# Three seams of a graph network kernel: first loads over other tiles between two stages, a new order in the third pass, and half of the head's sums kept in PSUM

## The chip, the core and the metric

One core of a Trainium2 chip runs the whole program. The metric is the device time of one execution in microseconds (us). The profile shows five engines beside each other: PE (TensorE, matrix products), DVE (VectorE), ACT (ScalarE), POOL (GpSimd) and SP (SyncE, which here only issues DMAs). PEld are PE's weight loads.

## What is computed

16 graphs of 1024 nodes with 128 channels pass two layers. The first layer runs four rounds of message passing with a GRU cell (`h = gru(adj.T @ (h @ W), h)`), adds the input and normalises each row. The second layer thins each adjacency by a row-by-row neighbour skipping, and runs three graph convolutions with a batch norm over all nodes of all graphs behind each of them:

```
adj_d = adj * keep(adj)                      # the skipping, row after row
def sage(x):  out = (adj_d @ x / deg) @ Wr + x @ Wx + b;  return out / norm(out) * mask
h1 = bn(relu(sage1(x)));  h2 = bn(relu(sage2(h1)));  h3 = bn(relu(sage3(h2)))
y  = (concat(h1, h2, h3) @ Wl + bl) * mask
out = layernorm(x + y)
```

Each batch norm needs all 16 graphs, so the convolutions are three passes over all graphs, and a head behind them.

## The kernel before

**First stage, to about 1334 us.** `Gated` (the GRU layer, two graphs in turn as two streams) and `FixPoint` (the skipping) run interleaved: `Gated.layer` calls `aside(n)` at fixed places, and each of these calls lets one piece of the skipping run. `Gated.layer` ends with the cell's last products: `zh = z*h` and `h = zh - r` on POOL (lines 1112, 1116, 1118) and a DVE step between them (L1117). After the last layer `finish` turns the state on PE (L1025), scales it on ACT (L1055), adds the input on POOL (L1057) and stores the sum from POOL's queue (L1059). The skipping leaves its rows in the DRAM tensor `e_nr`.

**First pass (`Sage.first`), about 1349 to 1900 us.** For each graph, 16 slots (`slot(b, t)`). A slot does one `unit` of the next graph n = b+1 (PE turns and combines pieces of the adjacency `p_a` and the skipping's rows `p_nr` into `p_u`, L1464 to L1471, and ACT evicts to `p_at`, L1472), a `pack` of it on POOL (L1479), and a share of the products of graph b (`agg`, L1543). Graph -1 is a lead-in: its 16 slots only prepare graph 0. `check` (L1488) looks at an adjacency tile on DVE; `norm_stats` and `norm` (L1497 to L1509) normalise the summed rows `p_s`, `turn_x` (L1402) turns them on PE, and `split` (L1396, L1397) cuts them in a high and a low part on ACT and POOL. Rows come by SP's queue: `load_a` (L1440), `load_nr` (L1448), `load_s` (L1454).

**Between them.** The constructor `Sage.__init__` loads weights, ten rows of vectors (L1228 to L1236) and three copies of the node mask (L1276), computes small constants on DVE and POOL, corrects the first weight by a product on PE (L1259), and turns the vectors (L1241). `run` then makes the first bias rows (`weights(0)`, L1344 and `parts`, L1320 to L1327) before `first` begins.

**Second pass**, to about 2171 us. **Third pass (`third`)**: 32 units of half a graph. In iteration i, `out_next(i)` makes three products on PE (L1734, L1737, L1740), `rows(i-2)` scales a result on DVE (L1386 to L1391), `chain(i)` scales on ACT (L1370), adds on DVE (L1373) and takes sums of squares on ACT (L1380, L1381), a DVE addition collects the head's part (L1833), and the result of i-3 is turned on PE (L1402), copied by ACT (L1837) and summed up by DVE's `bn_stats` (L1838).

**Head (`last`)**: `head_weights` makes one row `r48` for all graphs; for each graph, two halves of four products with the mask rows (L1864) and four with `r3` (L1867) in a PSUM tile; DVE adds `acc` (L1869), takes statistics (L1872, L1874), ACT a root (L1876), DVE the factors (L1881, L1882), and ACT writes eight normalised blocks (L1885) for one store of 512 KB (L1887). `norm(b-1)` comes after `head(b)`.

What sets the order: inside a stage the text of the program is the order of each engine's queue (`manual_schedule`); code outside of these sections, and two such sections towards each other, are placed by a planner. Tiles live in pools that are laid one behind the other in SBUF; a pool that opens over a closed one's space waits, tile by tile, for whoever still uses the old tiles there. DMAs of one queue are issued in order.

Of the kernel before, what the change touches and what calls it, by code (L numbers as in the profile page):

```python
# [21 lines left out]
P = 128  # L22
# [894 lines left out]
class Gated:  # L917
# [7 lines left out]
    def __init__(self, ctx, tc, cst, x, adj, weight, w_ih, w_hh, b_ih, b_hh, summed):  # L925
        self.tc, self.nc, self.cst = tc, tc.nc, cst
        self.x, self.adj, self.summed = x, adj, summed
        nc = self.nc
        pool = lambda name, **k: ctx.enter_context(tc.tile_pool(name=name, **k))
        self.one = pool("h_one", bufs=1)  # L930
        self.adjp = pool("h_adj", bufs=NB)
        self.wk = pool("h_wk", bufs=2)

        self.ps6 = pool("h_ps6", bufs=6, space=PSUM)
        self.wi = self.one.tile([C, L0, 3, C], F32, name="h_wi")
        self.wh = self.one.tile([C, L0, 3, C], F32, name="h_wh")
        self.bi = self.one.tile([C, L0 * 3], F32, name="h_bi")
        self.bh = self.one.tile([C, L0 * 3], F32, name="h_bh")
        self.bs = self.one.tile([C, L0 * 3], F32, name="h_bs")
        self.given = weight, w_ih, w_hh, b_ih, b_hh  # L940
# [50 lines left out]
    class Stream:  # L991
# [56 lines left out]
        def finish(self, f):  # L1048
# [8 lines left out]
            nc.gpsimd.tensor_tensor(x[:, rows, :], x[:, rows, :], y, ALU.add)  # L1057
# [3 lines left out]
    def layer(self, st, l, aside):  # L1061

        nc, wk = self.nc, self.wk
        half = [slice(f * HF, (f + 1) * HF) for f in range(2)]
# [28 lines left out]
        for f in range(2):  # L1093
# [17 lines left out]
            if f == 0:  # L1111
                nc.gpsimd.tensor_tensor(zh, z, h, ALU.mult)  # L1112
                aside(6)
        for f, (r, z, zh, h) in enumerate(rest):
            if f == 1:
                nc.gpsimd.tensor_tensor(zh, z, h, ALU.mult)
            nc.vector.scalar_tensor_tensor(r, z, 1.0, r, op0=ALU.subtract, op1=ALU.mult)  # L1117
            nc.gpsimd.tensor_tensor(h, zh, r, ALU.subtract)  # L1118
# [75 lines left out]
class Sage:  # L1194
# [14 lines left out]
    def __init__(self, ctx, tc, cst, adj, not_r, summed, nodemask, W, vec, Wl, bl, out, bad):  # L1209
        self.tc, self.nc, self.cst = tc, tc.nc, cst  # L1210
        self.adj, self.not_r, self.summed, self.out, self.bad = adj, not_r, summed, out, bad
        nc, ident = self.nc, cst["ident"]
# [10 lines left out]

        self.wr = one.tile([C, 3, C], F32, name="s_wr")
        self.wx = one.tile([C, 3, C], F32, name="s_wx")
        self.wl = one.tile([C, 3, C], F32, name="s_wl")
        for i in range(3):
# [3 lines left out]

        vr = one.tile([10, C], F32, name="s_vr")
        row = lambda v: v.rearrange("(o c) -> o c", o=1)
        for i, v in enumerate(vec):
            nc.sync.dma_start(vr[i:i + 1, :], row(v))
        nc.sync.dma_start(vr[9:, :], row(bl))  # L1236
        self.vr = vr
        self.vt = one.tile([C, 10], F32, name="s_vt")
        with tc.tile_pool(name="s_ps0", bufs=1, space=PSUM) as ps:
            pv = ps.tile([C, 10], F32, name="s_v")  # L1240
            nc.tensor.transpose(pv, vr, ident[:10, :10])  # L1241
            nc.vector.tensor_copy(self.vt, pv)
        const = lambda shape, v, name, dt=F32: self.const(shape, v, name, dt)
        self.eps = const([P, 1], 1e-5, "s_eps")
        self.less2 = const([P, 1], -2.0, "s_less2")
# [6 lines left out]
        with tc.tile_pool(name="s_wk1", bufs=1) as wk, tc.tile_pool(name="s_ps1", bufs=1, space=PSUM) as ps:  # L1252

            drop = wk.tile([C, C], F32, name="s_drop")
            nc.vector.tensor_copy(drop, ident)
            nc.vector.memset(drop[:1, :], -1.0)
            nc.vector.memset(drop[:1, :1], 0.0)
            w = ps.tile([C, C], F32, name="s_w1")
            nc.tensor.matmul(w, drop, self.wr[:, 0, :], start=True, stop=True)  # L1259
            nc.vector.tensor_copy(self.wr[:, 0, :], w)  # L1260
        self.part6 = one.tile([6, 3], F32, name="s_part6")
        nc.vector.tensor_add(self.part6, ident[:6, 0:3], ident[:6, 3:6])

        K = 3 * B
# [4 lines left out]
        self.graph = one.tile([K, B], F32, name="s_graph")  # L1269
        nc.vector.tensor_add(self.graph, ident[:K, :B], ident[:K, B:2 * B])  # L1270
        nc.vector.tensor_add(self.graph, self.graph, ident[:K, 2 * B:K])
        self.mask48 = one.tile([K, N], BF, name="s_mask48")
        with tc.tile_pool(name="s_wk0", bufs=1) as wk:
            m = wk.tile([K, N], F32, name="s_m48")
            for i in range(3):
                nc.sync.dma_start(m[i * B:(i + 1) * B, :], nodemask)  # L1276
            nc.vector.tensor_copy(self.mask48, m)
            o = wk.tile([B, N], BF, name="s_o16")
            nc.vector.memset(o, 1.0)
            for i in range(3):  # L1280
                nc.sync.dma_start(self.rho[:, 3 + i, :], o)

            junk = wk.tile([P, NB, B], F32, name="s_mjunk")
            mask = cst["mask"]
            nc.vector.scalar_tensor_tensor(junk, mask, 0.0, mask, op0=ALU.is_gt, op1=ALU.not_equal,
                                           accum_out=bad[:, BAD - 1:BAD])
        self.rdeg = one.tile([P, B, NB], F32, name="s_rdeg")
        self.stats = [one.tile([C, 2 * B, 6], F32, name=f"s_st{l}") for l in range(3)]
        self.ab = [one.tile([C, 2], F32, name=f"s_ab{l}") for l in range(3)]
        self.wr2 = one.tile([C, C], F32, name="s_wr2")  # L1290
        self.wxp = one.tile([C, 2, C], F32, name="s_wxp")
        self.r6 = one.tile([6, 2 * C], BF, name="s_r6")
        nc.vector.memset(self.r6[:, C:], 0.0)
# [35 lines left out]
    def weights(self, l, ps):  # L1329

        nc = self.nc
        v = ps.tile([6, C], F32, name="s_v6")
# [73 lines left out]
    def first(self):  # L1406

        nc, tc, cst = self.nc, self.tc, self.cst
        with ExitStack() as c:
            pool = lambda name, **k: c.enter_context(tc.tile_pool(name=name, **k))  # L1410
            self.wk = pool("p_wk", bufs=2)
            self.big = pool("p_at", bufs=2)
            self.ap = pool("p_a", bufs=8)
# [4 lines left out]
            c.enter_context(tc.manual_schedule(engines={ET.PE, ET.DVE, ET.Activation, ET.Pool, ET.SP}))  # L1418

            xp = pool("p_x", bufs=1)  # L1420
# [4 lines left out]
            self.g = {}  # L1425
            for k in range(4):
                self.load_a(0, k)
            for f in range(2):
                self.load_nr(0, f)
            self.load_s(0)  # L1430
            for k in range(4):
                self.check(0, k)
# [4 lines left out]
    def load_a(self, b, k):  # L1437
        if b < B:
            t = self.ap.tile([P, N], F32, name="p_a")
# [3 lines left out]
    def load_nr(self, b, f):  # L1443
        if b < B:
            g = self.g.setdefault(b, {})
            if f == 0:
                g["nr"] = self.big.tile([P, NB, N], BF, name="p_nr")
            self.nc.sync.dma_start(g["nr"][:, 4 * f:4 * f + 4, :], rows_of(self.not_r[b, f * HF:(f + 1) * HF, :]))  # L1448

    def load_s(self, b):  # L1450
        if b < B:
            g = self.g.setdefault(b, {})
            g["s"] = self.wk.tile([P, NB, C], F32, name="p_s")
            self.nc.sync.dma_start(g["s"], self.summed[b])  # L1454

    def unit(self, b, t):

        nc, g, f, j = self.nc, self.g[b], t // 8, t % 8
        if t == 0:
            g["at"] = self.big.tile([P, NB, N], FR, name="p_at")  # L1460
# [121 lines left out]
    def slot(self, b, t):  # L1582
# [4 lines left out]
        if nxt:  # L1587
            if t < 4:
# [52 lines left out]
        if nxt:  # L1641
# [6 lines left out]
            if t in (7, 12):  # L1648
                self.split_x(n, t // 12)
            if t in (4, 5, 10, 11):  # L1650
# [12 lines left out]
        if nxt:  # L1663
            if t == 10:
                nc.sync.dma_start(self.at8[n, 0], self.g[n]["b", 0])
            if t == 13:
                nc.sync.dma_start(self.x1[n], self.g[n]["s"])
        if t == 1 and b >= 1:
# [137 lines left out]
    def third(self):  # L1806

        nc, tc = self.nc, self.tc
        with ExitStack() as c:
# [10 lines left out]
            for i in range(len(units) + 3):  # L1820
                if i < len(units):
# [4 lines left out]
                if 2 <= i < len(units) + 2:  # L1826
                    b1, f1 = units[i - 2]
                    g = self.g[b1]
                    g["r", f1] = self.rows(b1, f1, g.pop(("o", f1)), g.pop(("ss", f1)))
                if i < len(units):  # L1830
# [3 lines left out]
                if i >= 3:  # L1834
                    b2, f2 = units[i - 3]
                    pt = self.turned(self.g[b2]["r", f2], self.ps2)
                    nc.scalar.copy(self.r3[:, b2, f2, :], pt)  # L1837
                    nc.vector.bn_stats(self.stats[2][:, 2 * b2 + f2, :], self.r3[:, b2, f2, :])  # L1838


    def last(self, r48):
        nc, tc, cst = self.nc, self.tc, self.cst
        with ExitStack() as c:
            pool = lambda name, **k: c.enter_context(tc.tile_pool(name=name, **k))
            wk = pool("u_wk", bufs=6)
            ps = pool("u_ps", bufs=4, space=PSUM)
# [3 lines left out]
            def row(b):  # L1850
                if b < B:
                    st["row", b] = wk.tile([3 * B, C], BF, name="u_rb", bufs=3)
                    nc.vector.tensor_scalar(st["row", b], r48, self.graph[:, b:b + 1], None, op0=ALU.mult)

            def head(b):
                rb = st.pop(("row", b))
                row(b + 1)
                y = wk.tile([P, NB, C], F32, name="u_y")
                mv = self.small.tile([P, NB, 2], F32, name="p_mv")
                for f in range(2):  # L1860
                    pp = ps.tile([P, 4, C], F32, name="u_p")
                    for i in range(4):
                        k = 4 * f + i
                        nc.tensor.matmul(pp[:, i, :], self.mask48[:, k * P:(k + 1) * P], rb,  # L1864
                                         start=(i == 0), stop=False)
                    for i in range(4):
                        nc.tensor.matmul(pp[:, i, :], self.r3[:, b, f, i * P:(i + 1) * P], self.wr2,  # L1867
                                         start=False, stop=(i == 3))
                    nc.vector.tensor_add(y[:, 4 * f:4 * f + 4, :], pp, self.acc[:, b, 4 * f:4 * f + 4, :])  # L1869
                    s6 = self.small.tile([P, 4, 6], F32, name="p_st")  # L1870
                    for i in range(4):
                        nc.vector.bn_stats(s6[:, i, :], y[:, 4 * f + i, :])  # L1872
# [4 lines left out]
                st[b] = y, mv, rs  # L1877

            def norm(b):
                y, mv, rs = st.pop(b)  # L1880
# [3 lines left out]
                for k in range(NB):  # L1884
                    nc.scalar.activation(y[:, k, :], y[:, k, :], AF.Identity, bias=rs[:, 1, k:k + 1],  # L1885
                                         scale=rs[:, 0, k:k + 1])
                nc.sync.dma_start(rows_of(self.out[b]), y)  # L1887

            row(0)
            for b in range(B + 1):  # L1890
# [5 lines left out]
    def run(self):  # L1896
        tc, nc = self.tc, self.nc
        with tc.tile_pool(name="s_psw", bufs=1, space=PSUM) as ps:
            self.weights(0, ps)
        self.first()  # L1900
        with tc.tile_pool(name="s_psw", bufs=1, space=PSUM) as ps:
            self.weights(1, ps)
# [4 lines left out]
        with tc.tile_pool(name="s_psw", bufs=1, space=PSUM) as ps:  # L1907
            self.weights(2, ps)
# [93 lines left out]
```

## Time and profile before

| what | us |
|---|---|
| median of 3 runs (2422.9 to 2429.3) | 2425.41 |
| the profiled execution | 2424.86 |
| its span, first to last instruction | 2423.1 |
| PE / DVE / ACT / POOL busy in it | 2260.7 / 1927.9 / 1384.0 / 1014.2 |
| mean granted clock of TensorE | 0.98 |

The page of the profile gives busy time by engine, 40 slices of the span, the chain of work that ended last, and groups by line. Other views answer questions on a stretch: a table by windows (busy time of each engine, granted clock, share and rate of the DMAs), a timeline (start, duration, engine, line, operation, and in brackets how long the engine had been idle before it and what ended that), and the waits. "x4" is four instructions merged in one line; a matrix product of 32-bit floats shows as two records. Times in the timeline count from the span's start.

### The profile page before, as it was taken

The numbers are of one execution on the slowest core, as the hardware profiler recorded it, in microseconds if no ns is written. First come the engines' busy times: TensorE is split into PE (matmuls) and PEld (weight loads), VectorE is DVE, ScalarE is ACT, GpSimd is POOL, SyncE is SP. The second block draws the span as 40 slices with busy tenths as digits, with TensorE's granted clock in tenths as the row PEclk, the third lists the DMA queues.
The fourth block names the chain that finished last, engine by engine and source line by source line (L and its number), as shares of the span: only waits on it lengthen the run. The fifth ranks groups of instructions, "written<-read, shape, count | busy, mean of one in ns | idle before, by whom it ended". The sixth has DMA issues, their size and how long they took to land.

```text
span 2423.1 us, 35665 instructions
## 1 busy us (share of the span) xinstructions
PE 2260.7 (93%) x11897; PEld 1558.2 (64%) x11913; DVE 1927.9 (80%) x4153; ACT 1384.0 (57%) x3228; POOL 1014.2 (42%) x937
## 2 busy tenths in 40 slices
PE   6999999999999999999998699999999899989875
PEld 4666555666556656566555477777777677777654
DVE  4998998989989989899899677777777466665677
ACT  3566556565565555565655466665666354545647
POOL 3335244353352442533523566666666244440000
PEclk9999999999999999999999799999999899999988
DMA  7337253364271643632722777887775466645404
GB/s 257 110 99 256 68 207 125 124 226 125 90 245 57 224 132 118 217 119 95 260 69 84 280 274 269 295 287 282 269 271 216 173 234 223 232 149 172 123 9 132
DMA packets 214389, 436.17 MB, mean 180 GB/s; under 512 B 59570, under 2 KB 80724, under 8 KB 214196
## 3 DMA queue, kind: packets, MB, share of 16 engines
q1 hardware_dynamic: 186756, 345.96, 41.5%
q0 software_dynamic: 23040, 83.90, 10.2%
q10 hardware_dynamic: 4400, 3.95, 0.5%
q8 instruction: 96, 1.57, 0.3%
q14 instruction: 97, 0.79, 0.1%
HBM read 324.49 MB, written 109.25 MB: 179 GB/s over the span
## 4 chain that ended last, share of the span: by engine, by line
PE 49%; DVE 22%; ACT 12%; DMA 8%; issue 6%; POOL 3%; SPq 0%; DVEq 0%; ACTq 0%; POOLq 0%
PE h_g L1089 12%; PE p_ag L1543 9%; PE h_g L1077 9%; DVE f_rank L735 4%; DMA e_sum<-h_x 3%; ACT s_junk L1380 2%; PE q_ag L1776 2%; PE p_u L1470 2%; PE p_u L1471 2%; PE p_u L1464 2%; ACT f_u L909 2%; DMA h_a<-in_adj_dram 2%; DVE f_x L893 2%; PE q_ob L1740 2%; PE s_tr L1402 1%
## 5 line engine op out<-in xcount | busy, mean ns | idle before, releaser
L1089 PE MATMUL h_g<-h_h,h_wh 128*128 128x512 f32 x768 | 397.7, 599 | 3.6 <-DVE h_r L1102 3.5
L1089 PE MATMUL h_g<-h_ms,h_wi 128*128 128x512 f32 x768 | 392.3, 592 | 0.0
L1479 POOL CAST p_b<-p_at 128x512 uint8<-128x512 f32 x256 | 256.3, 1021 | 129.5 <-ACT p_at L1472 129.4
L735 DVE TENSOR_TENSOR_SCAN f_rank<-f_a,f_first,f_pd 128x1024 f16<-128x1024 f32 x128 | 299.3, 2344 | 3.3
L1077 PE MATMUL h_g<-h_a,h_hi 128*128 128x512 f32 x1024 | 284.0, 417 | 7.5 <-DMA h_a<-in_adj_dram 7.4
L1118 POOL TENSOR_TENSOR h_h<-h_zh,h_r 128x512 f32<-128x512 f32 x128 | 184.7, 1443 | 198.1 <-DVE h_r L1117 170.7
L1472 ACT ACTIVATE p_at<-p_u,s_less 128x512 fp32r<-128x512 f32 x256 | 175.9, 688 | 157.9 <-PE p_u L1471 154.3
L1089 PEld LDWEIGHTS h_g<-h_ms,h_wi 128*128 128x128 f32 x768 | 145.5, 190 | 184.3 <-issue 164.2
L1077 PE MATMUL h_g<-h_a,h_lo 128*128 128x512 f32 x1024 | 262.0, 393 | 0.0
L1077 PEld LDWEIGHTS h_g<-h_a,h_hi 128*128 128x128 f32 x1024 | 188.3, 188 | 71.5 <-issue 20.3
L863 DVE SCALAR_TENSOR_TENSOR f_nr<-f_u,f_q,f_a 128x1024 bf16<-128x1024 f16 x128 | 183.8, 1453 | 57.1 <-ACT f_u L912 50.4
L1112 POOL TENSOR_TENSOR h_zh<-h_z,h_h 128x512 f32<-128x512 f32 x64 | 81.6, 1275 | 323.7 <-ACT h_z L1108 323.7
L1077 PEld LDWEIGHTS h_g<-h_a,h_lo 128*128 128x128 f32 x1024 | 189.9, 188 | 38.3
L1488 DVE SCALAR_TENSOR_TENSOR p_a<-p_a 128x1024 bf16<-128x1024 f32 x128 | 209.9, 1679 | 3.1 <-DMA p_a<-in_adj_dram 3.1
L1380 ACT ACTIVATE s_junk<-s_o 128x128 bf16<-128x128 f32 x384 | 113.7, 298 | 128.7 <-DVE s_o L1373 128.7
L1089 PEld LDWEIGHTS h_g<-h_h,h_wh 128*128 128x128 f32 x768 | 129.1, 190 | 86.7 <-issue 68.3
L1105 ACT ACTIVATE h_r<-h_r,h_bi 128x512 f32<-128x512 f32 x128 | 92.4, 722 | 140.8 <-DVE h_r L1104 140.8
L1080 ACT COPY h_ms<-h_g 128x512 f32<-128x512 f32 x128 | 73.9, 577 | 173.0 <-PE h_g L1077 129.9
L909 ACT ACTIVATE f_u<-f_rank,f_q 128x128 f16<-128x128 f16 (+7 forms) x128 | 110.6, 867 | 75.1 <-DVE f_rank L849 75.1
L1470 PE MATMUL p_u<-ident_b,p_a 128*128 128x128 bf16 x1024 | 144.9, 222 | 4.0 <-DMA p_a<-in_adj_dram 3.0
L1471 PE MATMUL p_u<-ident_b,p_nr 128*128 128x128 bf16 x1024 | 144.9, 222 | 0.0
L1740 PE MATMUL q_ob<-s_wxp,q_xt 128*128 128x256 f32 x512 | 130.8, 399 | 0.0
(243 smaller groups left out, 4942.2 us busy)
## 6 DMA issues: line engine op xcount, KB each, us to landing
h_a<-in_adj_dram POOLq DMA_DIRECT2D x128, 512.0 KB, 7.4
p_a<-in_adj_dram SPq DMA_DIRECT2D x128, 512.0 KB
f_a<-in_adj_dram SPq DMA_DIRECT2D x124, 512.0 KB
e_nr<-f_nr SPq DMA_DIRECT2D x128, 256.0 KB
p_nr<-e_nr SPq DMA_DIRECT2D x32, 1024.0 KB
s_at<-p_b SPq DMA_DIRECT2D x32, 512.0 KB
s_ag<-s_ag SPq DMA_DIRECT2D x64, 256.0 KB
q_agi<-s_ag SPq DMA_DIRECT2D x32, 512.0 KB
```

Of the source, the lines that this page charges most:

```text
L735: nc.vector.tensor_tensor_scan(out, a, other[:, 0, 0:1].to_broadcast([P, N]), start, op0=ALU.add, op1=ALU.bypass)
L863: nc.vector.scalar_tensor_tensor(nr, self.us[g], self.q[:, 2, g:g + 1], self.a[g], op0=ALU.not_equal, op1=ALU.is_ge)
L1077: nc.tensor.matmul(pm[f], part[:, j, :], st.adj[j][:, half[f]], start=(j == 0 and n == 0), stop=(j == NB - 1 and n == 1))
L1089: nc.tensor.matmul(pg, lhs, rhs, start=(i == 0), stop=(i == len(mm) - 1))
L1118: nc.gpsimd.tensor_tensor(h, zh, r, ALU.subtract)
L1470: nc.tensor.matmul(pu[:, i * P:(i + 1) * P], a[:, blk, 1], ib, start=False, stop=False)
L1471: nc.tensor.matmul(pu[:, i * P:(i + 1) * P], nr[:, k, blk], ib, start=False, stop=(i == 3))
L1472: nc.scalar.activation(g["at"][:, j, cols], pu, AF.Relu, bias=self.less2)
L1479: self.nc.gpsimd.tensor_copy(g["b", f][:, j, :], g["at"][:, j, f * HF:(f + 1) * HF].bitcast(F32))
L1488: self.nc.vector.scalar_tensor_tensor(low, a, 0.0, a, op0=ALU.is_gt, op1=ALU.not_equal, accum_out=self.bad[:, c:c + 1])
L1543: self.nc.tensor.matmul(pa, hi[:, j, :], at[:, j, f * HF:(f + 1) * HF], start=(start and n == 0), stop=(stop and n == len(js) - 1))
L1740: nc.tensor.matmul(pb[:, i], g["xt"][:, f, blk], self.wxp, start=False, stop=(i % 2 == 1))
```

## The change

Five things change. **(a)** `h_adj` is laid out ahead of `h_one`, and the pools of the first pass are split and ordered anew, so that the first rows' tiles (`p_nr0`, `p_a0`, `p_nr1`, `p_a1`) lie over the skipping's tiles and the rest over the adjacency of the GRU. The first loads stand at the head of `first` in one order on SP. **(b)** The constructor only makes tiles. Its loads stand behind the first rows (`load_given`); the constants come in the lead-in's slot 9 (`constants`), and the products with the weights, the vectors and `weights(0)` at the end of slot (0, 1) (`first_weights`). The first four `check`s move from ahead of the slots into slots 0 to 3 of the lead-in. **(c)** In the very last GRU layer, and in the last `finish`, POOL's products go to DVE (`aid`). **(d)** In the third pass the turn and copy of i-3 move ahead of `out_next(i)`, and its `bn_stats` between `rows` and `chain`. **(e)** In the head the products with `r3` come before those with the mask rows; the second half of each graph gets `acc` by a product with the identity, and its statistics and normalisation read PSUM; the row of each graph is made on POOL two graphs ahead; block 0 is normalised on POOL, and in the last graph blocks 2, 4 and 6 on DVE; eight PSUM tiles in place of four.

```diff
+        self.adjp = pool("h_adj", bufs=NB)
         self.one = pool("h_one", bufs=1)
-        self.adjp = pool("h_adj", bufs=NB)
...
+        aid = nc.vector if (st.b, l) == (B - 1, L0 - 1) else nc.gpsimd
-                nc.gpsimd.tensor_tensor(zh, z, h, ALU.mult)
+                aid.tensor_tensor(zh, z, h, ALU.mult)
-            nc.gpsimd.tensor_tensor(h, zh, r, ALU.subtract)
+            aid.tensor_tensor(h, zh, r, ALU.subtract)
...
+    def first_weights(self):
+        nc, ident = self.nc, self.cst["ident"]
+        bank = lambda: self.ps1.tile([P, 4, P], F32, name="s_tr")[:, 0, :]
+        w = bank()
+        nc.tensor.matmul(w, self.drop, self.wr[:, 0, :], start=True, stop=True)
+        nc.vector.tensor_copy(self.wr[:, 0, :], w)
+        v = bank()[:, :10]
+        nc.tensor.transpose(v, self.vr, ident[:10, :10])
+        nc.vector.tensor_copy(self.vt, v)
+        self.weights(0, bank()[:6, :])
+        nc.vector.tensor_copy(self.mask48, self.m48)
...
+            self.atp = [pool("p_at0", bufs=1)]
+            self.sp = pool("p_s", bufs=2)
+            xp = pool("p_x", bufs=1)
             self.wk = pool("p_wk", bufs=2)
-            self.big = pool("p_at", bufs=2)
-            self.ap = pool("p_a", bufs=8)
+            self.atp.append(pool("p_at1", bufs=1))
+            self.nrp, self.ap = [], []
+            for i in range(2):
+                self.nrp.append(pool(f"p_nr{i}", bufs=1))
+                self.ap.append(pool(f"p_a{i}", bufs=4))
...
+            self.load_nr(0, 0)
+            for k in range(4):
+                self.load_a(0, k)
+            self.load_nr(0, 1)
+            self.load_s(0)
+            for k in range(4, NB):
+                self.load_a(0, k)
+            self.load_given()
...
+            if t < 4 and not now:
+                self.check(n, t)
...
+        if (b, t) == (-1, 9):
+            self.constants()
+        if (b, t) == (0, 1):
+            self.first_weights()
...
             for i in range(len(units) + 3):
+                if i >= 3:
+                    b2, f2 = units[i - 3]
+                    pt = self.turned(self.g[b2].pop(("r", f2)), self.ps2)
+                    nc.scalar.copy(self.r3[:, b2, f2, :], pt)
                 if i < len(units):
...
+                if i >= 3:
+                    nc.vector.bn_stats(self.stats[2][:, 2 * b2 + f2, :], self.r3[:, b2, f2, :])
                 if i < len(units):
                     pp = self.chain(b, f, True)
                     acc = self.acc[:, b, 4 * f:4 * f + 4, :]
                     nc.vector.tensor_add(acc, pp, acc)
-                if i >= 3:
-                    b2, f2 = units[i - 3]
-                    pt = self.turned(self.g[b2]["r", f2], self.ps2)
-                    nc.scalar.copy(self.r3[:, b2, f2, :], pt)
-                    nc.vector.bn_stats(self.stats[2][:, 2 * b2 + f2, :], self.r3[:, b2, f2, :])
...
+                    if f:
+                        nc.tensor.matmul(pp.rearrange("p a b -> p (a b)"), cst["ident"],
+                                         acc.rearrange("p a b -> p (a b)"), start=False, stop=False)
...
+                    if not f:
+                        nc.vector.tensor_add(y[:, :4, :], pp, acc)
+                    src = pp if f else y
```

## The prediction

> **What bounds it now.** I read the 40 slices first: PE is at nine tenths almost everywhere, except around 1330 us and in the last 250 us. Then the table by windows (us, busy time and count of PE, PEld, DVE, ACT, POOL; granted clock, DMA share, GB/s):
>
> ```profile
> 1326.00:1349.00 23.00, 3.85 (x13) 2.20 (x13) 15.65 (x40) 3.58 (x10) 12.22 (x9) 0.58 0.52 177
> 1349.00:1375.00 26.00, 17.99 (x161) 14.11 (x162) 17.22 (x41) 13.90 (x22) 17.17 (x15) 0.76 1.00 371
> 1375.00:1409.00 34.00, 33.51 (x261) 26.35 (x261) 22.78 (x58) 19.81 (x48) 21.67 (x24) 0.96 0.71 257
> 2220.00:2330.00 110.00, 92.65 (x556) 71.53 (x554) 72.11 (x169) 72.69 (x342) 0.00 (x0) 0.98 0.30 88
> 2355.00:2410.00 55.00, 37.76 (x314) 30.93 (x312) 53.59 (x288) 47.62 (x125) 0.00 (x0) 0.99 0.41 125
> ```
>
> PE works 3.85 of 23 us at the seam; the lead-in behind it is full of DMA (share 1.00, 371 GB/s); graph 0 is PE-bound (33.51 of 34). In the third pass (fourth row) nobody is full; in the head (fifth) DVE is. The chain of waits and the timelines say what each waits for:
>
> ```profile
> 1340.08 2.95 DMA e_sum<-h_x
> 1343.18 0.40 SPq L1448 DMA_DIRECT2D p_nr<-e_nr  x1
> 1349.10 0.58 PE L1464 MATMUL p_u<-p_nr,ident_b 128*128 128x512 bf16 x1 [8.67 <-DMA p_nr<-e_nr]
> 1354.94 0.87 DVE L1497 BATCH_NORM_STATS2 p_st<-p_s 128x6 f32<-128x128 f32 x4 [4.13 <-DMA p_s<-e_sum]
> 1374.79 0.29 PE L1470 MATMUL p_u<-ident_b,p_a 128*128 128x128 bf16 x1 [2.98 <-DMA p_a<-in_adj_dram]
> ```
>
> The first skipping rows are not loaded until the GRU's last store has left its tile (1340.08 + 2.95); SP is in order, so the sums and the other rows follow late too.
>
> **Seam (a, b, c).** e_nr's last store is issued by 1319.95, and the f_rank and f_a tiles, over which the new pools lie by my sum of tile sizes, were last read at 1319.8 (ACT L886) and 1319.6 (DVE L863). So SP can start at about 1321 (1323 if it must wait for e_nr to land). Ahead of the sums stand 1 + 2 + 1 MB, with them 4.5 MB: at 371 to 390 GB/s 12 us, landing near 1334.5 (before: 1354.9); 3 MB, enough for unit 0, land near 1331. PE's last GRU turn began at 1333.58, after POOL's 2.19, 1.70 and 1.28 (L1118, L1116, L1118). On DVE, whose products of this shape take 0.68 (L1117, 1327.48): the skipping's check ends near 1325.5, L1102 and L1104 take 1.3, ACT's tanh and z 1.3, then three products 1.9 to 1330.0; the turn ends near 1331. The price: the first zh waits on DVE for ACT's z (to 1322.4), with the skipping's check (L893, L879) queued behind it; that took 4.9 beside POOL in before and about 2.4 alone. So unit 0 goes at 1331.5, not 1349.1.
>
> Then DVE sets the pace. From 1334.5 it has, to the end of `first_weights`: statistics of two graphs 4 x 1.07, eight norms 2.6, roots and reciprocals with their waits 1.6, twelve checks at 1.25 to 1.67 (alone, and beside POOL's casts, at 1361 and 1363) 15 to 20, constants about 3 (L1297 to L1293 took 2.7, L1279 0.91 in before), and the round trips 1.4: 28 to 33 us, so 1362.5 to 1367.5. The loads give nearly the same for slot (0, 0): 11.6 MB from 1321.5 at 390 GB/s end at 1353. The 20 issues of `load_given` take SP 0.23 to 0.63 each (1328.92 to 1335.7 and 1343.7 to 1345.1 in before), 8 us together, ahead of graph 1's rows; those are needed at 1353 only, and graph 0's 2 MB keep the DMAs busy meanwhile. `first_weights` is a new wait: three products share one PSUM tile, and PE stands in order behind DVE's copies, with slot (0, 2) behind it; I take 1366.2 (5 to 6 us of standing). In before unit 2 of that slot began at 1380.68. Gain 14.5; DVE's backlog (`parts` 2.3, the mask's cast 0.69) makes the sums of slot 6 about 1 late: **13.5**. Bounds: 19 if PE does not stand, 8 if DVE and POOL slow each other as where L1117 took 1.75 for 0.68. `h_adj` first means that the kernel's first row loads wait for the node mask's tile: 3.04 becomes about 4.3 to 5.3, while weights and f_a fill the queues; DMA is 0.9 full to 26 us, so I take 0 (-1 to +2).
>
> **Third pass (d).** One unit takes 4.56 us:
>
> ```profile
> 2262.07 0.57 ACT L1837 COPY s_r<-s_tr 128x512 f32<-128x512 f32 x1
> 2262.53 1.15 ACT L1370 ACTIVATE s_o<-q_oa,s_rdeg 128x128 f32<-128x128 f32 x4
> 2262.67 0.69 DVE L1838 BATCH_NORM_STATS2 s_st<-s_r 128x6 f32<-128x512 f32 x1 [1.46 <-ACT s_r L1837]
> 2264.49 0.68 DVE L1373 TENSOR_TENSOR s_o<-q_ob,s_o 128x512 f32<-128x512 f32 x1
> 2264.71 0.63 PE L1402 MATMUL s_tr<-ident,s_r 128*128 128x128 f32 x4 [0.57 <-DVE s_r L1391]
> 2265.20 0.31 ACT L1380 ACTIVATE s_junk<-s_o 128x128 bf16<-128x128 f32 x1 [1.52 <-DVE s_o L1373]
> ```
>
> It is a ring: ACT's copy 0.60, DVE's bn_stats 0.61, rows 1.21, addition 0.71, ACT's squares and root 1.43 = 4.56. ACT idles 1.52 in it and DVE 1.46. With the copy of i-3 at the head of i and bn_stats behind `rows`, `rows` (1.21) is done while ACT takes squares, and bn_stats while ACT scales. What is left: copy 0.46, scaling 1.23 with its wait, addition 0.71, squares 1.43 = 3.83. PE alone needs 3.79 (turns at 2200.39 and 2204.18, with nothing between that waits); its turn of i-3 needs `rows` of the iteration before, which are done 0.4 after ACT's copy starts, so PE is just filled. I take 3.87: 28 units x 0.69 = 19.3, less 0.4 for the turn that now comes ahead of the fourth unit, and the drain behind the last addition (9.1 now) gets about 2 shorter: **21**. Bounds: 24 (PE's 3.79), 14 (4.1, if ring and PE wait for each other).
>
> **Head (e).** DVE is full, 3.98 us a graph: two halves of addition 0.69, statistics 0.79 + 0.28, then 0.20 + 0.09 + 0.16.
>
> ```profile
> 2356.52 0.39 PE L1864 MATMUL u_p<-u_rb,s_mask 48*128 48x128 bf16 x4
> 2356.84 1.16 PE L1867 MATMUL u_p<-s_wr,s_r 128*128 128x128 f32 x8
> 2382.73 0.24 DVE L1853 TENSOR_SCALAR u_rb<-s_r,s_graph 48x128 bf16<-48x128 bf16 x1
> 2410.62 6.26 ACT L1885 ACTIVATE u_y<-u_y,u_rs 128x128 f32<-128x128 f32 x16
> ```
>
> One addition (0.69) and the row (0.16) leave DVE: 3.13. ACT loses one block of eight: about 3.0. PE, back to back 1.41 a half (2355.11 to 2356.52), gains a 32-bit product of 512 columns: six of them took 5.15 at 1316.92, so 0.86, and PE becomes the bound at 3.69. The early products with r3 need only the scaled weights (2339.6), not r48 (2343.3), but PE runs there at half pace (0.60 for 0.39), and the identity product costs twice as much: about even by graph 1. Fifteen graphs x 0.28 = 4.2; at the end ACT has 7 + 4 blocks in place of 16, 2.0 less; DVE has less to do behind PE's last product, 0.9: **7**. Statistics from PSUM have no row of this shape; an addition from PSUM (L1373) takes 0.69 and a product from SBUF alone (L1117) 0.68, so 0; the upper bound, 0.1 for each of four, still leaves DVE below 3.69. POOL's row and block are bounded by its 1.27 for 512 columns, so at most 0.9 together, two graphs and one root ahead of their readers.
>
> [...] No row of this trace shows a statistic of 128 elements from PSUM.
>
> **Sum.** 13.5 + 21 + 7 = 41.5; 2424.86 - 41.5 = 2383.4, and with the 0.55 by which the median lies above the profiled execution, **2384**. A measurement of this kernel can tell 0.3% (7.3 us) from no change.
>
> **Rivals.**
> - *The seam is given back* (17%): one of the new pools lies over a GRU tile that the last store still reads, and SP, in order, stops again until about 1341, or PE stands longer in `first_weights`. For it: SP stopped so in before. Against: the tile sizes. Seam 0 instead of 13.5: 2397.
> - *A new wait in the third pass* (12%): PE now meets the turn at the head of its queue, and three products are behind it; if `rows` come late, unit time stays near 4.5. For: PE already waited 0.57 there. Against: `rows` no longer stand behind bn_stats. Third pass 2: 2403.
> - *More than forecast* (10%): PE does not stand at slot (0, 1), units take 3.79, DVE's end is shorter: 19 + 24 + 8: 2374.
> - *Slower* (4%): one mechanism, the granted clock. Third pass and head become PE-full; at clock c they take 28 x 3.79/c + 14 x 3.69/c against 28 x 4.56 + 14 x 3.98, and the seam and the ends give about 19. So it decides below c = 0.78; at 0.70 the time is about 2448. Against: first stage and first pass are PE-full at 1.00 and 0.96.
> - *No change that shows* (3%): seam and third pass fail together, 7 or less left: 2418 to 2425.
>
> The forecast has 54%, 2372 to 2395 by itself. Adding the first two rivals, the range is 2370 to 2405. Faster by over 0.3%: 0.93; within: 0.03; slower: 0.04.
>
> **What would show it.** First `p_nr` issue near 1321 and unit 0 near 1331; sums landing near 1334; PE idle 5 us in slot (0, 1), ended by DVE; `p_ag` of slot (0, 2) 13 to 15 earlier; turns of the third pass 3.8 to 3.9 apart with ACT nearly full; heads 3.7 apart with PE full and DVE idle; eleven blocks at ACT's end. It is wrong if SP's first load is issued after 1335, if units stay above 4.2, or if DVE is still full in the head.

## The result, and the profile after

The changed kernel takes **2398.2 us** (2395.4 to 2399.7, 4 runs) against 2426.4 (2422.9 to 2429.3, 4 runs) beside it: ratio 0.9883, 95% interval 0.9866 to 0.9900. It is faster by 28 us where 41.5 were forecast; 2398 lies inside the range (2370 to 2405), 14 above the predicted 2384, but outside the 2372 to 2395 that the forecast had by itself. The profiled execution took 2395.37 with a span of 2393.6. Cut at four landmarks of the two traces, the 29.5 us between the spans are:

| stretch | before | after | gain | forecast |
|---|---|---|---|---|
| start to the first product of the third pass | 2184.19 | 2182.13 | 2.1 | 13.5 |
| from there to the first product of the head | 159.44 | 134.50 | 24.9 | 21 |
| from there to the last normalised block | 73.25 | 67.40 | 5.9 | 7 |
| behind that block | 6.25 | 9.61 | -3.4 | 0 |

So the third pass and the head did what was forecast, almost nothing of the seam's gain is left, and a loss at the very end had not been thought of. One landmark moved with the edit: the head's first product is one with the mask rows before and one with `r3` after. Before, it came 2.39 behind the last product of `head_weights`, now 0.79; so 1.6 of the 24.9 belong to the head's new order, and the third pass itself gained 23.3. The table by windows (us, busy time and count of PE, PEld, DVE, ACT, POOL; granted clock, DMA share, GB/s) shows the seam in five rows, then the third pass and the head:

```profile
1326.00:1340.00 14.00, 7.00 (x54) 5.22 (x55) 7.73 (x27) 6.12 (x13) 2.19 (x4) 0.68 1.01 388
1340.00:1349.00 9.00, 8.62 (x96) 6.72 (x94) 9.00 (x13) 7.67 (x14) 8.46 (x8) 0.92 0.35 104
1349.00:1356.00 7.00, 1.35 (x13) 0.64 (x10) 6.92 (x16) 1.62 (x3) 6.55 (x11) 0.93 1.04 404
1356.00:1361.00 5.00, 0.79 (x4) 0.26 (x4) 4.70 (x9) 0.00 (x0) 0.02 (x1) 0.50 0.49 142
1361.00:1368.00 7.00, 1.66 (x7) 1.20 (x8) 3.85 (x7) 0.69 (x1) 0.07 (x1) 0.50 0.97 355
2220.00:2305.00 85.00, 85.00 (x537) 71.10 (x537) 69.26 (x156) 67.54 (x315) 0.00 (x0) 1.00 0.40 113
2320.00:2371.00 51.00, 51.00 (x356) 36.01 (x356) 43.47 (x257) 34.59 (x97) 12.76 (x25) 0.99 0.38 115
```

PE is full in the third pass and in the head. At the seam it works only until 1349: the lead-in is through some 21 us earlier than before (its last unit starts at 1349.4, before at 1370.4), and then PE stands for most of 15 us, in which the granted clock falls to 0.50. The DMAs move 388 and 404 GB/s in two of the rows, but 104 GB/s from 1340 to 1349 and 142 from 1356 to 1361. SP's timeline (start, duration of the issue, line) tells why (lines count in each kernel's own text; L1458, L1466 and L1472 are `load_a`, `load_nr` and `load_s` here):

```profile
1316.73 0.37 SPq L1466 DMA_DIRECT2D p_nr<-e_nr  x1
...
1326.34 1.02 SPq L1248 DMA_DIRECT2D s_wr<-in_L_gnn_Wr_dram  x1
1328.52 0.33 SPq L1249 DMA_DIRECT2D s_wx<-in_L_gnn_Wx_dram  x1
1332.29 0.33 SPq L1248 DMA_DIRECT2D s_wr<-in_L_gnn_Wr_dram  x1
...
1345.84 0.97 SPq L1466 DMA_DIRECT2D p_nr<-e_nr  x2
1346.85 0.50 SPq L1472 DMA_DIRECT2D p_s<-e_sum  x1
1347.47 1.14 SPq L1458 DMA_DIRECT2D p_a<-in_adj_dram  x2
1357.56 1.25 SPq L1290 DMA_DIRECT2D s_rho<-p_rl  x3
1358.91 0.37 SPq L1458 DMA_DIRECT2D p_a<-in_adj_dram  x1
...
1359.84 0.38 SPq L1458 DMA_DIRECT2D p_a<-in_adj_dram  x1
```

The first load goes out at 1316.73. But `load_given` keeps SP from 1326.34 to 1345.8, and only then graph 1's skipping rows (L1466) are issued: the first hole. Three stores (L1290) stand from 1348.6 to 1357.56 ahead of graph 1's third adjacency row: the second hole. The waits of SP between 1325 and 1346 (line, what ended them, us in total, times, longest):

```profile
SPq L1248 <- DMA p_a<-in_adj_dram: 3.7, 2, 2.6
SPq L1248 <- DMA p_nr<-e_nr: 3.4, 1, 3.4
SPq L1249 <- DMA p_a<-in_adj_dram: 2.7, 2, 1.6
SPq L1249 <- DMA p_s<-e_sum: 1.0, 1, 1.0
```

Small loads into tiles that nobody uses wait until large loads ahead of them have landed.

What they wait for is a rule of this program: in the instruction records of the trace the issues of SP and ACT share eight semaphores (counters that an issue waits on and a landing raises). On SP's queue they take turns (919 of 932 issues use the one that the eighth issue before used), and these issues wait on the semaphore that they then use. Ahead of `load_given` stand 11 large loads (one `p_nr`, four `p_a`, one `p_nr`, the sums, four `p_a`), and its first issues waited for the fourth, fifth, sixth and so on of them: they stand at 1326.34, 1328.52, 1332.29 and 1333.59, and the eighth load before each landed at 1326.33, 1328.50, 1332.27 and 1333.57. Its vectors and masks could go only when graph 0's last row had landed, at 1340.97. Whether the queue by itself would have taken more is not shown.

The three stores waited for DVE, which writes their source. DVE's timeline, and POOL's:

```profile
1350.58 0.29 DVE L1280 SCALAR_TENSOR_TENSOR p_rl<-mask 128x128 f32<-128x128 f32 x1
...
1350.80 5.30 DVE L1284 COPY p_rl<-ident 128x128 f32<-128x128 f32 x1
...
1356.62 0.91 DVE L1288 MEMSET p_rl<- 16x1024 bf16 x1 [0.16 <-issue]
```

```profile
1350.87 1.71 POOL L1497 CAST p_b<-p_at 128x512 uint8<-128x512 f32 x3
1352.55 1.25 POOL L1406 TENSOR_TENSOR p_xl<-p_s,p_xh 128x508 fp32r<-128x508 f32 x1
1353.74 2.27 POOL L1497 CAST p_b<-p_at 128x512 uint8<-128x512 f32 x4
```

A copy of 128 columns took 5.30 us, where the operation ahead of it, of the same size, took 0.29. From 1350.87 to 1356.01 POOL ran eight operations without a pause, and the copy ended 0.1 later. PE's timeline closes the account (in brackets the idle time ahead of the product, and what ended it): the last of graph 1's first four rows lands at 1366.7.

```profile
1363.63 0.29 PE L1488 MATMUL p_u<-ident_b,p_a 128*128 128x128 bf16 x1 [4.18 <-DMA p_a<-in_adj_dram]
1366.74 0.29 PE L1488 MATMUL p_u<-ident_b,p_a 128*128 128x128 bf16 x1 [2.72 <-DMA p_a<-in_adj_dram]
```

Third pass, one unit (turns start at 2263.26 and 2267.05): ACT still waits 0.76 in the ring and DVE 0.35, and PE waits for nothing.

```profile
2263.26 0.60 PE L1411 MATMUL s_tr<-ident,s_r 128*128 128x128 f32 x4
2263.53 0.69 DVE L1382 TENSOR_TENSOR s_o<-q_ob,s_o 128x512 f32<-128x512 f32 x1 [0.35 <-ACT s_o L1379]
2264.25 0.31 ACT L1389 ACTIVATE s_junk<-s_o 128x128 bf16<-128x128 f32 x1 [0.76 <-DVE s_o L1382]
2267.05 0.60 PE L1411 MATMUL s_tr<-ident,s_r 128*128 128x128 f32 x4
```

Head: the mask products that end a graph's second half begin at 2366.35, 2370.04 and 2373.73, 3.69 apart. The end of the program (the first line is from before):

```profile
2411.45 0.19 PE L1926 MATMUL l_sum<-l_col,l_max 128*1 128x1 f32 x2 [5.58 <-DVE l_max L1922]
...
2383.58 0.46 ACT L1925 ACTIVATE u_y<-u_p,u_rs 128x128 f32<-128x128 f32 x1 [0.48 <-DVE u_y L1923]
2384.09 0.19 PE L1964 MATMUL l_sum<-l_col,l_max 128*1 128x1 f32 x2 [6.27 <-ACT u_y L1925]
```

`l_sum` adds up the marks that `check` has set; all five engines load the flag made of it (from 2384.5 on, 0.47 to 0.57 each) and branch. Before, it ran 5.4 us ahead of the end of the last block; now it waits for that block.

### The profile page after: what moved, and what is told of

It reads as the page before. It is cut to its first block, busy times and chain, and to the rows that moved or that the text cites. A ratio compares the mean times of both kernels' runs of the same rounds, so it can differ in the third digit from the quotient of the medians.

```text
span 2393.6 us, 35727 instructions
## 1 busy us (share of the span) xinstructions
PE 2269.3 (95%) x11945; PEld 1561.1 (65%) x11945; DVE 1924.3 (80%) x4130; ACT 1373.5 (57%) x3209; POOL 1014.7 (42%) x963
## 3 DMA queue, kind: packets, MB, share of 16 engines
q0 software_dynamic: 23040, 83.90, 10.2%
## 4 chain that ended last, share of the span: by engine, by line
PE 58%; DVE 16%; ACT 10%; DMA 9%; issue 4%; POOL 3%; SPq 0%; DVEq 0%; ACTq 0%; POOLq 0%
PE h_g L1092 15%; PE h_g L1080 12%; PE p_ag L1561 9%; DMA e_sum<-h_x 3%; DVE f_rank L735 3%; ACT s_junk L1389 3%; PE q_ag L1800 3%; PE p_u L1482 2%; PE p_u L1489 2%; PE p_u L1488 2%; DMA h_a<-in_adj_dram 2%; PE q_ob L1764 2%; PE s_tr L1411 1%; DVE s_o L1382 1%; PE u_p L1890 1%
```

## The experiments

**Theory:** the seam's gain is lost where graph 1's rows are issued, in the two holes of SP's queue. **Rivals:** DVE's backlog and `first_weights` gate the seam in any case; DMA throughput alone does. One yardstick serves all kernels: the time from the start of the GRU stage's last product with adjacency rows (`h_g<-h_a`) to the start of three products: the last of the GRU's last turn, the first of `agg` (its tiles are `p_ag`), and the first of `agg` for graph 1. Each time is compared with the kernel before on the same chip. The expectations speak of 24 loads in `load_given`; it issues 20 (7 of matrices, 10 vectors, 3 masks).

| kernel | GRU's last turn | first `p_ag` | first `p_ag` of graph 1 | time, us (range) | ratio to before, 95% |
|---|---|---|---|---|---|
| before | 19.9 | 60.6 | 95.5 | 2426.4 (2422.9 to 2429.3) | |
| tail_only | 19.9 | 60.9 | 96.1 | 2399.7 (2398.7 to 2400.2) | 0.9875 to 0.9908 |
| changed | 15.5 | 55.6 | 94.3 | 2398.2 (2395.4 to 2399.7) | 0.9866 to 0.9900 |
| after_again | 15.8 | 54.8 | 92.9 | 2398.8 (2394.5 to 2400.6) | 0.9863 to 0.9894 |
| flag_early | 15.5 | 55.0 | 92.6 | 2394.6 (2392.0 to 2397.3) | 0.9858 to 0.9891 |
| drop_stt | 15.5 | 55.7 | 94.3 | 2397.1 (2395.1 to 2397.7) | 0.9865 to 0.9898 |
| rho_late | 15.5 | 52.2 | 91.0 | 2393.5 (2390.3 to 2397.1) | 0.9845 to 0.9878 |
| drop_act | 15.5 | 51.8 | 90.4 | 2391.2 (2390.4 to 2397.9) | 0.9844 to 0.9886 |
| nr_first | 15.5 | 51.1 | 88.7 | 2392.6 (2391.0 to 2396.6) | 0.9849 to 0.9885 |
| given_act | 15.5 | 47.5 | 92.1 | 2395.5 (2393.7 to 2398.9) | 0.9861 to 0.9896 |
| all_act | 15.8 | 48.2 | 92.4 | 2393.7 (2390.9 to 2396.7) | 0.9853 to 0.9887 |
| no_aid | 17.3 | 51.0 | 88.8 | 2393.5 (2392.5 to 2396.3) | 0.9849 to 0.9879 |
| best_a | 15.8 | 52.2 | 89.9 | 2391.5 (2390.6 to 2393.2) | 0.9841 to 0.9871 |
| best_b | 15.8 | 53.5 | 89.6 | 2386.6 (2385.2 to 2390.8) | 0.9819 to 0.9846 |

Four profiles share the changed kernel's seam (changed, after_again, flag_early, drop_stt) and give 92.6 to 94.3; the two with the old seam 95.5 and 96.1. So the yardstick scatters by up to 1.8 us, and the seam itself gained 2.2 in the mean. Part of that is given back at the next seam, which the yardstick does not see: from the last `p_ag` product to the second pass's first product (`q_oa`) it is 4.4 and 4.5 us in the two kernels with the old seam, and 5.7 to 6.0 in all twelve with the new one; in the changed kernel that product waits for the end of `parts`, in before it does not. Why is not shown.

**Third pass and head alone** (`third` and `last` as changed, everything else as before).

> The kernel before with only the third pass and the head of the change (its parts d and e); the seam, the first rows' pools and the GRU's last layer are as before. If the parts add, as the landmarks of the two traces say (third pass 23.2, head to the last write 7.6, given back after the last write 3.35), it takes about 2426.4 - 27.4 = 2399, so that the whole seam (and the 1.7 us at the start) is worth 1 to 2 us. The rival (the seam's 4 us at the last slots of the first pass are real and the third pass gains less by itself, because it ran at another clock or beside other DMA): 2402 to 2406.

2399.7: the parts add as the landmarks say, and the whole seam is worth 1.5 us, less than can be told from nothing.

**The stores of ones behind the rows.**

```diff
-        for i in range(3):
-            nc.sync.dma_start(self.rho[:, 3 + i, :], o)
+        if (b, t) == (-1, 11):                      # in slot, behind load_a(1, 3)
+            for i in range(3):
+                nc.sync.dma_start(self.rho[:, 3 + i, :], self.o16)
```

> The changed kernel with one thing moved: the three stores of the vector of ones (s_rho<-p_rl) are issued at the end of slot 11 of the lead-in instead of slot 9, behind the issues of a(1,2), of the first at8 store and of a(1,3). Main theory (the seam's gain is held on SP's queue: a(1,2) and a(1,3) stood behind stores that waited for DVE until 1357.5): a(1,3) is issued at about 1351 instead of 1359.8, the rows of graph 1 land near 1359 (then limited by the 3.5 MB issued just ahead of them), the first p_ag product falls from 1366.9 to about 1359.5, and most of that stays: about 5 to 7 us off 2398, some 2392. Rival A (DVE's backlog gates the seam anyway, through the weights of slot (0,1)): the first p_ag product is earlier but first_weights then stands for as long, and the time stays within 1.5 us of 2398. Rival B (the rows are limited by DMA throughput alone): a(1,3) is issued early, lands no earlier than 1364, gain under 2.5 us.

The row is issued at 1351.25, 8.6 earlier (10.4 by the yardstick, since the GRU ended 1.8 later here), but lands at 1365.2 (3.3 earlier by the yardstick), as rival B had it. The line of the chain of waits (start, us, what):

```profile
1351.25 13.94 DMA p_a<-in_adj_dram
```

With the row itself 5 MB were issued from 1347.5 on; from 1350 on the DMAs were full, at 375 to 418 GB/s. The first `p_ag` comes 3 earlier by the yardstick, of the theory's 7; the time fell by 5, which is the theory's and not rival B's, but the intervals overlap. Both holes count: with the second closed, the limit is what the first has put off.

**The slow copy in another form, and on another engine.**

```diff
-        nc.vector.tensor_copy(drop, ident)
+        nc.vector.scalar_tensor_tensor(drop, ident, 0.0, ident, op0=ALU.max, op1=ALU.mult)   # drop_stt
+        nc.scalar.copy(drop, ident)                                                           # drop_act, on rho_late
```

> The changed kernel with one DVE instruction in another form: drop = ident is written by a scalar_tensor_tensor (max 0, times ident: the same values) instead of a copy. Theory (the copy of 128x128 f32 stands 5.30 us because this form can't run beside POOL's casts, as the checks in scalar_tensor_tensor form do in 1.3 to 2.4 us at 128x1024): the instruction takes 0.3 to 0.6 us, the memset of the ones ends at about 1352.7, the rho stores are issued near 1352.8 and a(1,3) near 1355; the first p_ag product falls by 4 to 5 us to about 1362 and the time by 3 to 5 us, to 2394. Rival (any DVE instruction put there stands behind POOL's run, whatever its form): it takes 5 us as well and nothing moves (within 1 us).

> The kernel of rho_late with the copy drop = ident done by ACT instead of DVE. It tells whether DVE's 5.3 us stall costs anything once the rows don't stand behind it. Theory (DVE stood because POOL ran seven instructions without a pause): DVE's backlog ends about 5 us earlier (the memset of ones near 1353 instead of 1359.2), no other DVE instruction takes its place in the stall by more than 2 us; since the rows land at 1365 anyway, the time stays within 1.5 us of rho_late (2393). Rival (DVE's backlog is still what first_weights and the slots behind it wait for): 3 to 5 us faster, 2389.

In drop_stt it took 5.37: the other form stalls as well. In drop_act the stall was not gone but moved to the next check, which took 5.04 in place of 1.3; my "no other takes its place" was wrong. No cost shows there: the stores of ones were through ahead of it, and 2391 against 2393 is inside the scatter.

**The order of the loads** (both on rho_late): graph 1's `p_nr` and `p_s` ahead of `load_given`, or all of `load_given` on ACT's queue.

```diff
+            for f in range(2):                      # nr_first, in first()
+                self.load_nr(1, f)
+            self.load_s(1)
             self.load_given()
...
-            nc.sync.dma_start(self.wr[:, i, :], W[2 * i])
+            nc.scalar.dma_start(self.wr[:, i, :], W[2 * i])        # given_act, and all others of load_given
```

> The kernel of rho_late with the loads of graph 1's skipping rows and sums (p_nr, p_s) issued ahead of the 24 loads of weights, vectors and masks instead of behind them. Theory (in rho_late the rows of graph 1 landed at 1365.2 though a(1,3) was issued at 1351.3, because p_nr could only be issued at 1347.5, behind those 24 issues, while the DMA engines moved under 100 GB/s from 1342 to 1350): p_nr is issued before 1335, the 2.5 MB go into that hole, graph 1's last row of the first four lands near 1358, first p_ag at about 1358 against 1365.4, and the time falls by 5 to 7 us below rho_late, to 2387. Rival (the time is set by DVE's backlog and first_weights behind the rows): the first p_ag product comes early but PE stands as long in slot (0,1), time within 1.5 us of rho_late, 2393. Second rival (the weights now come late: first_weights waits for W): same time, with PE waiting for s_wr or s_vr.

> The kernel of rho_late with all 24 loads of weights, vectors and masks issued by ACT's queue instead of SP's. Theory as for nr_first: SP issues p_nr before 1335, graph 1's first four rows land at 1353 to 1358, first p_ag 1354 to 1358, time 5 to 9 us below rho_late, 2385 to 2388. Its own cost: ACT issues for some 7 us from about 1328 on, ahead of the first two units' evictions and of p_rs; it was idle for 5 of the 7 us there, so 1 to 2 us at most, on a stretch in which the units wait for rows anyway. Rival: ACT's issues are held back like SP's by the DMA queue until 1340, the first evictions with them, unit 15 ends some 8 us later and the gain is gone: 2393 or more.

nr_first: `p_nr` is issued at 1325.4, and the DMAs move 330 GB/s from 1342 to 1346. But the 20 small loads now end at 1351.7, and graph 1's first four adjacency rows go out behind them, so that the hole lies from 1346 to 1354 (55 and 118 GB/s). The last row lands at 1361.4. Graph 1 comes 2.3 earlier than in rho_late; the time differs by 1, which can't be told. given_act: graph 1's last row was used at 1359.7, but ACT was held up in its issues until 1339.5, with the first evictions behind them (10.2 us idle): its issues share the eight semaphores with SP's, so that a small load of ACT stood until 1337.2 for SP's `p_nr`, and SP's load of the sums until 1334.2 for ACT's `s_wl`. The gain at the first `p_ag` (4.7 on rho_late) is gone at graph 1. PE's wait in slot (0, 1), and POOL at the same time:

```profile
1372.22 0.27 PE L1298 MATMUL s_tr<-ident,s_vr 10*128 10x10 f32 x1 [5.76 <-DVE s_wr L1296]
```

```profile
1360.87 9.50 POOL L1495 CAST p_b<-p_at 128x512 uint8<-128x512 f32 x2 [0.43 <-ACT p_at L1488]
```

Here the rival holds: with the rows there, `first_weights` stands behind DVE's backlog, which ran from 1361.9 to 1371.4 without a pause. Rows and DVE's backlog are two limits a few us apart.

> rho_late, given_act, drop_act and flag_early together. If they add: 2398.2 - 4.7 (rho_late) - 6 (given_act) - 1 (drop_act, whose stall then is on PE's path) - 3.5 (flag_early) = about 2383. If the seam is gated by something none of them touches: 2390.

They don't add: 2393.7, near the "gated by something else" of 2390. The seam is given_act's.

**The GRU's last products back on POOL** (`aid = nc.gpsimd` in both places, part (c) undone).

> The changed kernel with the last GRU layer's products and the last additions back on POOL. Theory (unit 0 was early, but the units stood from 1331 to 1337 for the sums and graph 0's other rows, so that the GRU's earlier end was not on the path): the GRU's last turn comes 4 to 5 us later relative to its last product with h_a (20 us instead of 15.5), unit 15 and the first p_ag product less than 1.5 us later, and the time stays within 1.5 us of the changed kernel. Rival (the GRU's end sets the lead-in): first p_ag and time 4 us later, 2402.

The GRU ends only 1.8 later by the yardstick, and the first `p_ag` comes about 4 *earlier*; 2393.5 against 2398.8 beside it, with intervals that overlap. Both expectations were wrong: by this one profile, part (c) costs. POOL and DVE meet at other places in the lead-in, and the copy takes

```profile
1352.80 0.62 DVE L1284 COPY p_rl<-ident 128x128 f32<-128x128 f32 x1
```

so that DVE's constants take 5.3 (1349.46 to 1354.78) in place of 8.0. By the yardstick the stores leave SP 4.3 earlier and the last row 4.1 (1357.35), which is the first `p_ag`'s gain. Why the two engines met less badly is not shown; it is a matter of a few us of order, and another kernel may have it the other way.

**The flag inside the head**: its reduction, product and test during graphs 1 to 3, in a bank of its own, `u_ps` with 7.

```diff
+                if b in (1, 2, 3):
+                    self.flag(b, lp)                # reduce; l_sum; l_flag
                 if b:
                     norm(b - 1)
```

> The changed kernel with the flag's sum and test computed inside the head, during graphs 1 to 3, in a PSUM bank of its own (u_ps has 7 instead of 8), so that only the load of the flag and the branch stay behind the last graph. Theory (after the last u_y the changed kernel loses 3.35 us, since the flag's product can't start before ACT has read the last PSUM bank, and every engine's branch, with its fetch of instructions, follows it): from the last u_y to the end 6.2 us as in the kernel before instead of 9.6, so about 2395. Rival (the end is the 6 us of the last store plus the branch of SP, whatever the flag): no change beyond 0.5 us. A cost: the head's PE takes 0.2 us more, and one bank less could hold PE up by as much as 0.1 us per graph, 1.6 us in all.

From the last block to the end 6.77 instead of 9.61, and the time is 3.6 below the changed kernel's, with intervals that overlap. In the four profiles with this edit the end takes 6.75 to 6.80, in the nine others with the new head 9.31 to 9.63. So 2.8 of the 3.4 lost are shown to be the branch's wait; whether the shared bank or the place in the program put `l_sum` last was not separated.

**Together.** best_a is nr_first, drop_act and flag_early; best_b also does `first_weights` in the lead-in:

```diff
-        if (b, t) == (0, 1):
+        if (b, t) == (-1, 15):
             self.first_weights()
+            for k in range(4):
+                self.check(1, k)
```

> nr_first, drop_act and flag_early together (rho_late is in the first two): graph 1's skipping rows and sums ahead of the weights' loads, the stores of ones behind the rows, drop copied by ACT, the flag inside the head. If they add to the changed kernel's 2398.2: seam -6 (nr_first), a further -1 (DVE's backlog 4 to 5 us shorter, so that unit 2 of slot (0,2) goes 42 us behind the GRU's last turn instead of 43.0), end -3.5: 2388. If nr_first and drop_act take the same microseconds twice: 2389 to 2390.

> best_a with first_weights (three small products of PE and DVE's copies between them) moved from slot (0,1) to the end of the lead-in, where PE stands for graph 1's rows, and with the checks of graph 1's first four rows behind it on DVE. Theory (in slot (0,1) PE stands 4 to 5 us in first_weights, behind DVE): unit 2 of slot (0,2) comes 3 to 4 us earlier relative to the GRU's last turn than in best_a, time 2385. Rival (PE's standing there only replaces what the rows and DVE's checks would cost, so it moves to the next wait): within 1.5 us of best_a, 2388.

> The changed kernel once more, beside the three others: 2398, between 2395 and 2400. It gives them a comparison on the same chip.

best_a gives 2391.5, no more than nr_first or drop_act alone. **best_b gives 2386.6**, 0.5% below the changed kernel on the same chip, with intervals apart (0.9819 to 0.9846 against 0.9863 to 0.9894): it beats both kernels. Its profiled execution was its slowest (2390.8) and shows no earlier graph 1 than best_a, with the 5-us stall on a check in the lead-in (5.05 at 1352.63). The theory's ground was missing too: in best_a PE stood only 0.39 and 0.26 in `first_weights`. So where its 5 us below best_a come from is not shown, and the intervals of the two just overlap.

## Why the prediction was right or wrong

- **Seam, the early steps:** right, and on the safe side. First load 1316.7 (forecast 1321), sums used at 1333.6 (1334.5), unit 0 at 1328.4 (1331.5), the last product of the GRU's last turn at 1326.8 (end near 1331). The rival that the pools lie over a GRU tile fell.
- **Seam, the failed step:** "11.6 MB from 1321.5 at 390 GB/s end at 1353". The rate was right, but not that it is kept up: the last row landed at 1366.7. Two terms were missing. "The 20 issues of `load_given` take SP 8 us together" came from rows with few loads under way; behind graph 0's 11 large loads they took 19.5, since each waits for the landing of the eighth load before it, which I had not seen. And of the moved `constants` I priced DVE's part only: its three stores stand on SP's queue ahead of graph 1's rows, and wait for DVE. rho_late and nr_first show that each of the two put graph 1's rows off.
- **Seam, DVE:** constants "about 3" took 8.0, for the 5.3 us of one instruction beside POOL. I had bounded that by "DVE and POOL slow each other", at 1.75 for 0.68. PE's standing in `first_weights` (5 to 6 us) did not occur, since PE was standing for rows; it came back (5.8) where the rows came early.
- **The rival "given back"** is what happened, by another mechanism than its two: seam 0 and the rest as forecast made 2397. That the time came out so near is partly luck: 2.3 more than forecast in the third pass and 1.6 at the head's start stand against 3.4 lost behind the last block.
- **(c):** its gain at the GRU's end was real (4.4), but from unit 4 on PE then stood 5.2 (to 1337.9) behind ACT, whose queue waited for the statistics of the sums; I had it on the path. By no_aid's profile it cost some 4 at the first `p_ag`.
- **`h_adj` first:** first product of the first stage at 33.9 against 35.6. Over all profiles it lies between 32.3 and 37.2, so 0 within the bounds taken.
- **Third pass:** right. A unit takes 3.79, PE's own time, where 3.87 was taken; the ring has 0.35 to 0.76 to spare, so PE, not the ring, sets it. Without the 1.6 of the head's new order the gain is 23.3 here and 21.7 in tail_only, between the forecast and the upper bound of 24.
- **Head:** 3.69 a graph, exactly PE's sum. PE's whole run gained only 1.0 of the 4.2, since the first graph takes PE 5.8 in place of 3.69, mostly at a granted clock of 0.50 (eight products in 2.05 for 1.16). Before, these products were as slow (2.07), but DVE set the pace. DVE and ACT behind the last product gained 4.8 instead of 2.9. Four statistics from PSUM took 0.89 against 0.87 from SBUF: 0.02 a graph, where the prediction took 0, with 0.1 for each as the bound.
- **Behind the last block:** I stopped at the last block. The flag's product was hidden behind ACT's 16 blocks before; once they got shorter and it came last, its branch did too: 3.4.

## What to carry to other kernels

A moved block of "constants" is also the DMAs that it issues: write down for each queue what stands behind them and which engine they wait for. A sum of bytes over a rate holds only while the queue can be fed (388 and 404 GB/s here while it was, 104 and 142 around the two holes): check that each large load is issued before the one ahead of it has landed, count how many DMAs the program lets be under way (eight here, for two queues together), and put small loads that nobody needs yet behind the large ones that somebody waits for (nr_first: 2.3 us earlier at graph 1, though no difference in time that can be told). When a stage's tail gets shorter, look again at what used to be hidden behind it, to the last instruction of the program.

## What had not been expected of the hardware

- DVE and POOL held each other up over whole runs of instructions. DVE's copy or a check behind it took 5.04 to 5.32 in the profiles of changed, rho_late, given_act, drop_act and best_b beside a row of eight POOL operations, and the copy's other form 5.37 in drop_stt; in no_aid's the copy took 0.62, another operation of its size took 0.29, and checks with POOL idle 1.27 to 1.32 (changed, from 1357.46 on). Two POOL casts took 9.50 while DVE ran checks in a row (given_act). At other places of the same lead-in neither stood for that long: four checks of the changed kernel took 1.38 to 2.40 each beside POOL's operations. What decides whether one stands is not shown. In those stalls the copy ended 0.1 behind POOL's last operation (changed, rho_late, given_act) and the check 1.15 behind it (drop_act, best_b), so neither was through between two instructions of POOL's run.
- Two waits look like the hardware's, but the trace has them as waits on semaphores, so that the program asks for them: the small DMA issues behind large ones (19.5 us for 20), and the last blocks of the head, where DVE and ACT read the same PSUM tile and each waited for the other's block (2.50 on DVE, 0.48 on ACT). Whether the chip needs either was not tried.
